# Group norm of layer 1 put ahead of the block turns on VectorE, its 1/std applied by ScalarE

## The chip, the cores and the metric

The kernel runs on one core of a Trainium2 chip. A core has five engines that each work through a queue of their own in order: TensorE (PE, matrix products; PEld is its weight load, which overlaps), VectorE (DVE), ScalarE (ACT), GpSimd (POOL) and SyncE (SP, which issues most transfers here). [...] The metric is the device time of one execution in microseconds; the median of 3 runs of the kernel before is 3231.37 us (3231.11 to 3235.41).

## What is computed

Two attention layers over an image x of 128 rows, 256 columns and 256 channels (with a batch of one). Each layer adds to x an attention over the columns of each row, computed from a group norm of x. Cut to what matters here:

```
def _gn(v, G=32, eps=1e-5):            # statistics over rows, columns and the 8 channels of a group
    g = v.reshape(B_, H_, W_, G, C_ // G)
    m = jnp.mean(g, axis=(1, 2, 4), keepdims=True)
    s = jnp.var(g, axis=(1, 2, 4), keepdims=True)
    return ((g - m) / jnp.sqrt(s + eps)).reshape(v.shape)

x = x + _L0_conv_ref(_gn(x), ...)      # 8 heads, layer norm, pair bias from z, gate
x = x + _L1_conv_ref(_gn(x), ...)      # 4 heads, scores only where |i - j| <= 16

def _L1_conv_ref(x, w_in, b_in, w_out, b_out, band):
    qkv = x2 @ w_in.T + b_in
    q, k, v = jnp.split(qkv, 3, axis=-1)
    ...                                # scores, softmax inside the band, times v
    return (out @ w_out.T + b_out).reshape(B, T, F, C)
```

The group norm of layer 1 needs mean and variance over the whole output of layer 0. So layer 1 can't begin its products before the last row of layer 0 is done: that point is the seam.

## The kernel before

Both layers go over the 128 rows in 64 pairs. Layer 0 stores its result in 16 blocks of 8 rows (`x1[j]`, stored from the tile `xo`, L1456, 2 MB each) and gathers the moments of each block on VectorE (L1471 to L1484) into `st1`, which holds mean and summed squares by partition and group.

Layer 1 works on one pair at a time, transposed, with channels on the partitions. For each pair four transfers on SP's queue bring `xs` (L1771) in such an order that a single VectorE transpose of 32x32 blocks turns it into `xT` (method `turn`, L1781); a fifth brings the rows as they are (`xt`, L1776) for the residual. `centre(k)` (L1786, on ScalarE, one for each half `k` of the channels) subtracts the mean and writes `xgT`, on which PE's products work; with the second half POOL adds the output bias to `xt` (L1788). The transfers of a pair are issued where its object is made, not where its methods are called.

At the seam, `norm1` makes the constants of the norm: VectorE spreads the group's mean over its channels (L1723), PE averages over the partitions (L1724), VectorE forms the variance (L1725 to L1727), PE turns mean and variance into columns with channels on partitions (L1732), VectorE adds eps and negates the mean (`R1c` L1736, `nM1` L1738), POOL raises to the power -1/2 (L1737). VectorE then multiplies `R1c` into the input weights `w_in`, six instructions (L1742): 1/std is applied through the weights, the mean through the data.

`mix_weights` (L1749 to L1752, POOL) forms four sums of blocks of the q and k weights, `wst`. The pairs from the second on compute q and k with seven products of 128x128 blocks in place of eight; `wst` is for these products (`product`, L1824), together with four sums of data, `dT`, which `differences` (L1795 to L1798, POOL) makes from `xgT`. The first pair is projected in the plain way (`project`, L1845).

The seam is written out by hand, and each engine takes its instructions in this order: both pairs made (their transfers issued), `now.turn()`, `nxt.turn()`, `norm1()`, the two `now.centre(k)`, `mix_weights()`, then four projections, two rows of values, `nxt.centre(k)` and `nxt.differences()`. After it comes the loop over the pairs; its first pass begins with `nn.turn()` for the third pair, and each pass ends with `n3.turn()`, the turn for two passes ahead. The tiles `wst`, `xs`, `xT`, `xgT` and `gn_each` lie in memory that layer 0 has used; `w_in`, `nM1` and `st1` are constants that stay in place.

Of the kernel before, what the change touches and what calls it, by code (L numbers as in the profile page):

```python
# [9 lines left out]
F32 = mybir.dt.float32  # L10
AF = mybir.ActivationFunctionType
ALU = mybir.AluOpType
# [4 lines left out]
P = 128  # L17
# [4 lines left out]
def bcast(ap, axis, n):  # L22

    ap = ap.unsqueeze(axis)
    shape = list(ap.shape)
    shape[axis] = n
    return ap.broadcast_to(shape)
# [746 lines left out]
def fast_kernel(  # L774
# [25 lines left out]
    nc = tc.nc  # L800
    S, I, C = x.shape
# [7 lines left out]
    KC = C // P  # L809
# [6 lines left out]
    const = ctx.enter_context(tc.tile_pool(name="const", bufs=1))  # L816
# [17 lines left out]
    def load_chunks(src, n, name):  # L834
        t = const.tile([P, src.shape[0] // P, n], F32, name=name)
        queued.append((t, src.rearrange("(k p) n -> p k n", p=P)))
        return t
# [90 lines left out]
    w_in = load_chunks(w_inT, 3 * C, "w_in")  # L928

    w_out = const.tile([P, KC, C], F32, name="w_out")  # L930
    for a in range(KC):
        for h in range(H1):
            n = P // H1
# [5 lines left out]
    for h in range(H1):  # L939
        n = P // H1  # L940
# [279 lines left out]
    class Pair:  # L1220
# [36 lines left out]
        def centre(self):  # L1257
            self.xg = la.tile([P, NT, C], F32, name="xg", tag="xg", bufs=1)
            nc.gpsimd.tensor_tensor(self.xg, self.xt, bcast(M0, 1, NT), ALU.subtract)
# [303 lines left out]
    behind, nx, n = None, 0, 0  # L1563
# [41 lines left out]
    with tc.manual_schedule():  # L1605
# [3 lines left out]
        for p in range(NP):  # L1609
# [52 lines left out]
            old, was, now, nxt, nn = was, now, nxt, nn, nn3  # L1662
# [41 lines left out]
    with tc.tile_pool(name="l1", bufs=2) as sb, tc.tile_pool(  # L1704
        name="l1s", bufs=4
    ) as sm, tc.tile_pool(name="ps1_s", bufs=4, space=PSUM) as ps_s, tc.tile_pool(
        name="ps1_o", bufs=1, space=PSUM
    ) as ps_o:

        def mm1(name):  # L1710
            return ps_s.tile([P, 512], F32, name=name, tag="s")

        nM1 = const.tile([P, KC], F32, name="nM1")
        wst = sb.tile([P, 4, 2, P], F32, name="wst", bufs=1)

        def norm1():

            each = sm.tile([P, 2, C], F32, name="gn_each", bufs=1)
            dev = sm.tile([P, C], F32, name="gn_dev", bufs=1)
            R1c = sm.tile([P, KC], F32, name="gn_R", bufs=1)  # L1720
            ps = [mm1("ps_gn") for _ in range(2)]
            by_group = lambda a: a.rearrange("p (g e) -> p g e", e=GE)
            nc.vector.tensor_copy(by_group(each[:, 0, :]), bcast(st1[:, :, 1], 2, GE))  # L1723
            nc.tensor.matmul(ps[0][:, :C], avg, each[:, 0, :], start=True, stop=True)  # L1724
            nc.vector.tensor_tensor(dev, each[:, 0, :], ps[0][:, :C], ALU.subtract)  # L1725
            nc.vector.tensor_mul(dev, dev, dev)
            nc.vector.scalar_tensor_tensor(  # L1727
                by_group(each[:, 1, :]), bcast(st1[:, :, 2], 2, GE), 1.0 / (S * NB * GE), by_group(dev), ALU.mult, ALU.add
            )
            for n in range(2):  # L1730
                for k in range(KC):
                    nc.tensor.matmul(  # L1732
                        ps[1][:, 2 * n + k : 2 * n + k + 1], each[:, n, k * P : (k + 1) * P], avg[:, 0:1],
                        start=True, stop=True,
                    )
            nc.vector.tensor_scalar_add(R1c, ps[1][:, 2:4], 1e-5)  # L1736
            nc.gpsimd.tensor_tensor(R1c, R1c, mhalf[:, :KC], ALU.pow)  # L1737
            nc.vector.tensor_scalar_mul(nM1, ps[1][:, 0:2], -1.0)  # L1738
            for n in range(3):
                for k in range(KC):  # L1740
                    at = slice(n * C, (n + 1) * C)
                    nc.vector.tensor_scalar_mul(w_in[:, k, at], w_in[:, k, at], R1c[:, k : k + 1])  # L1742

        def mix_weights():

            a = [[w_in[:, k, 0 : 2 * C].rearrange("p (n m c) -> p m n c", n=2, m=KC)[:, m] for k in range(KC)]
                 for m in range(KC)]
            s1, s2, s3, s4 = (wst[:, n] for n in range(4))
            nc.gpsimd.tensor_tensor(s1, a[1][0], a[1][1], ALU.add)  # L1749
            nc.gpsimd.tensor_tensor(s2, s1, a[0][0], ALU.subtract)  # L1750
            nc.gpsimd.tensor_tensor(s3, a[0][0], a[1][0], ALU.subtract)
            nc.gpsimd.tensor_tensor(s4, a[0][1], s2, ALU.subtract)  # L1752
# [9 lines left out]
        class Pair1:  # L1762
# [20 lines left out]
            def centre(self, k):  # L1783
                if k == 0:
                    self.xgT = sb.tile([P, KC, N2], F32, name="xgT1", tag="xgT")
                nc.scalar.activation(self.xgT[:, k, :], self.xT[:, k, :], AF.Identity, bias=nM1[:, k : k + 1])  # L1786
                if k == KC - 1:
                    nc.gpsimd.tensor_tensor(self.xt, self.xt, bcast(bout_r, 1, 2 * NB), ALU.add)  # L1788

# [167 lines left out]
        def pair1(p):  # L1957
            return Pair1(p) if p < NP else Nobody()
# [14 lines left out]

        with tc.manual_schedule():
            now, nxt = pair1(0), pair1(1)
            now.turn()
            nxt.turn()
            norm1()
            for k in range(KC):
                now.centre(k)  # L1980
            mix_weights()
            for m in range(KC):
                now.project("qT", m)
                now.project("kT", m)
            for r in range(2):
                now.values(r)
            for k in range(KC):
                nxt.centre(k)
            nxt.differences()
# [6 lines left out]
        with tc.manual_schedule():  # L1996
            was = Nobody()
            for p in range(NP - 1):
# [42 lines left out]
                was, now, nxt = now, nxt, nn  # L2041
# [19 lines left out]
        ps = mm1("ok_ps")  # L2061
# [4 lines left out]
@with_exitstack  # L2066
def mixer_kernel(ctx, tc, *args):

    nc = tc.nc
    keep = ctx.enter_context(tc.tile_pool(name="verdict", bufs=1))  # L2070
    verdict = keep.tile([1, 1], mybir.dt.int32, name="verdict")
    fast_kernel(tc, *args, verdict)
    again = nc.values_load(verdict[0:1, 0:1], min_val=0, max_val=1)
    with tc.If(again > 0):
        general_kernel(tc, *args)
# [53 lines left out]
```

## Time and profile before

| | before |
|---|---|
| median of 3 runs | 3231.37 us (3231.11 to 3235.41) |
| profiled execution, its own time | 3251.55 us |
| its span, first to last instruction | 3249.8 us |
| busy in the span | PE 95%, DVE 72%, POOL 66%, ACT 47% |
| mean granted PE clock | 0.982 |
| last block of layer 0 stored (x<-xo issued, landed) | 2051.12, 2058.18 us |
| first projection of layer 1 on PE | 2078.93 us |
| first scores of layer 1 on PE | 2090.88 us |

Times of single instructions count from the start of the span. A line of the profile names the engine, the line of the kernel, the operation and the tiles (written `out<-in`, with buffer numbers and trailing digits left out: `nM` is `nM1`, `xs<-x` is a load from `x1`); `xN` counts instructions that stand merged. In brackets stands how long the engine was idle before, and who released it. The profiled execution took 20.2 us more than the runs' median, so differences are formed within the profile and carried over to the median.

### The profile page before, as it was taken

To read this page: it belongs to the slowest core of one execution; us is meant where nothing else is said; L and a number is where in the kernel's file an instruction comes from. 1 tells how busy PE (TensorE), PEld (TensorE's weight loads), DVE (VectorE), ACT (ScalarE), POOL (GpSimd) and SP (SyncE) were. 2 spreads that over 40 slices of the span, in tenths; PEclk is the share of its full clock that TensorE was granted. 3 is DMA by queue.
4 is the path that set the end of the run, shared out by engine and by line. 5 is a ranking of instruction groups with operands and counts; after the bars stand their busy time and mean duration, and the time that the engine had idled before them with its cause. 6 is when DMAs were issued, how large, how long until landed. Compare 5 with 4: busy or idle time off the path is not lost.

```text
span 3249.8 us, 82756 instructions
## 1 busy us (share of the span) xinstructions
PE 3073.5 (95%) x34916; PEld 2066.9 (64%) x34916; DVE 2339.4 (72%) x3684; ACT 1537.5 (47%) x2501; POOL 2157.6 (66%) x1631
## 2 busy tenths in 40 slices
PE   5379999999999999999999999699999999999998
PEld 3245555555555555555555555488888888888886
DVE  7966676777777777777777777577766666666676
ACT  2255444444444444444444444255555555555553
POOL 3368888888888887888788886355454555545453
PEclk9799999999999999999999999899999999999999
DMA  9953333434433442344343332533334334343431
GB/s 349 391 150 63 65 88 86 95 70 96 95 95 70 95 91 64 87 92 95 70 95 96 67 88 70 106 80 89 92 88 92 91 90 95 85 100 86 94 93 47
DMA packets 726973, 329.10 MB, mean 101 GB/s; under 512 B 574560, under 2 KB 675808, under 8 KB 725440
## 3 DMA queue, kind: packets, MB, share of 16 engines
q1 hardware_dynamic: 721520, 320.81, 40.3%
q8 instruction: 277, 4.54, 0.7%
q10 hardware_dynamic: 5072, 2.90, 0.3%
q14 instruction: 104, 0.85, 0.1%
HBM read 254.88 MB, written 68.75 MB: 100 GB/s over the span
## 4 chain that ended last, share of the span: by engine, by line
PE 71%; DMA 12%; DVE 8%; POOL 4%; issue 2%; ACT 1%; SPq 1%; ACTq 0%; DVEq 0%; POOLq 0%
PE ps_p L1322 13%; PE ps_qk L1824 11%; PE ps_v L1860 7%; PE ps_su_y L1943 7%; PE ps_sc L1356 6%; PE ps_y L1443 5%; PE ps_ov L1388 5%; PE ps_v L1337 5%; PE ps_o L1903 3%; DMA rvb<-rsum 3%; PE ps_sc L1874 3%; DMA rs_d<-lrs 3%; DMA rsum<-rv 3%; PE ps_su L1396 2%; POOL eboth L1377 2%
## 5 line engine op out<-in xcount | busy, mean ns | idle before, releaser
L1377 POOL TENSOR_TENSOR eboth<-e 128x512 f32<-128x512 f32 x512 | 639.4, 1272 | 214.8 <-DVE e L1372 214.7
L1363 ACT ACTIVATE ps_sc<-ps_sc 128x1024 f32<-128x1024 f32 x512 | 492.8, 1006 | 575.9 <-PE ps_sc L1356 575.9
L1372 DVE TENSOR_TENSOR e<-ps_sc,eb 128x1024 f32<-128x1024 f32 x512 | 602.9, 1219 | 221.8 <-ACT ps_sc L1363 219.2
L1885 POOL TENSOR_TENSOR e<-e,bw 128x384 f32<-128x384 f32 x256 | 252.7, 1008 | 520.3 <-ACT e L1883 520.3
L1356 PE MATMUL ps_sc<-qT,kT 32*128 32x256 f32 x4096 | 293.3, 400 | 2.0 <-ACT kT L1326 2.0
L1443 PEld LDWEIGHTS ps_y<-wo,oT 128*128 128x128 f32 x1024 | 190.8, 190 | 106.6 <-POOL oT L1433 51.1
L1443 PE MATMUL ps_y<-wo,oT 128*128 128x256 f32 x1024 | 246.2, 383 | 12.8 <-POOL oT L1433 11.5
L1322 PE MATMUL ps_p<-xnT,wq 128*128 128x512 f32 x512 | 254.8, 619 | 2.6 <-POOL xnT L1309 2.3
L1309 POOL TENSOR_TENSOR xnT<-xgT,rs_r 128x512 f32<-128x512 f32 x128 | 160.1, 1273 | 135.4 <-DMA rs_r<-rs_d 133.2
L1943 PE MATMUL ps_su_y<-w_out,oT 128*128 128x256 f32 x1024 | 245.9, 384 | 3.8 <-DVE odd L1921 2.8
L1337 PE MATMUL ps_v<-wv,xnT 128*128 128x256 f32 x1024 | 248.6, 386 | 0.0
L1388 PE MATMUL ps_ov<-e,v 128*32 128x256 f32 x4096 | 247.7, 382 | 0.0
L1356 PEld LDWEIGHTS ps_sc<-qT,kT 32*128 32x128 f32 x4096 | 184.9, 184 | 94.4 <-issue 82.6
L1829 ACT ACTIVATE u<-ps_qk,bin_c 128x256 f32<-128x256 f32 x378 | 177.7, 478 | 141.2 <-PE ps_qk L1824 133.2
L1322 PE MATMUL ps_p<-xnT,wk 128*128 128x512 f32 x512 | 240.6, 592 | 0.0
L1860 PE MATMUL ps_v<-w_in,xgT 128*128 128x256 f32 x1024 | 238.3, 386 | 0.0
L1337 PEld LDWEIGHTS ps_v<-wv,xnT 128*128 128x128 f32 x1024 | 189.3, 190 | 76.8 <-issue 56.9
L1322 PE MATMUL ps_p<-xgT,wg 128*128 128x512 f32 x512 | 236.8, 605 | 0.0
L1922 DVE RECIPROCAL rv<-odd 128x256 f32<-128x256 f32 x128 | 224.4, 1753 | 4.4
L1943 PEld LDWEIGHTS ps_su_y<-w_out,oT 128*128 128x128 f32 x1024 | 196.4, 192 | 32.3 <-DVE odd L1921 3.6
L1860 PEld LDWEIGHTS ps_v<-w_in,xgT 128*128 128x128 f32 x1024 | 189.3, 190 | 32.8 <-issue 0.5
L1824 PE MATMUL ps_qk<-dT,wst 128*128 128x256 f32 x756 | 191.4, 389 | 5.2 <-DVE qT L1835 5.1
(198 smaller groups left out, 5694.3 us busy)
## 6 DMA issues: line engine op xcount, KB each, us to landing
xa<-in_x_dram SPq DMA_DIRECT2D x8, 4096.0 KB
xt<-in_x_dram SPq DMA_DIRECT2D x64, 512.0 KB
x<-xo SPq DMA_DIRECT2D x16, 2048.0 KB
xs<-x SPq DMA_DIRECT2D x256, 128.0 KB
xt<-x SPq DMA_DIRECT2D x64, 512.0 KB
xs<-in_x_dram SPq DMA_DIRECT2D x252, 128.0 KB
rvb<-rsum SPq DMA_DIRECT2D x252, 128.0 KB
out_dram<-yo SPq DMA_DIRECT2D x63, 512.0 KB
```

What stands on the lines that cost most here:

```text
L1322: nc.tensor.matmul(ps, w[:, k, m * P : (m + 1) * P], getattr(self, src)[:, k, :], start=(k == 0), stop=(k == KC - 1),)
L1337: nc.tensor.matmul(self.ps_v[:, b * C : (b + 1) * C], self.xnT[:, k, t * P : (t + 1) * P], wv[:, k, :], start=(k == 0), stop=(k == KC - 1),)
L1356: nc.tensor.matmul(self.pss[q // 2][:, q % 2, b, :], self.kT[rs, c, r * I + b * P : r * I + (b + 1) * P], self.qT[rs, c, r * I : (r + 1) * I],
L1363: nc.scalar.activation(self.pss[a], self.pss[a], AF.Exp)
L1372: nc.vector.tensor_tensor(e, pss[a], eb[:, h : h + 2], ALU.mult)
L1377: nc.gpsimd.tensor_tensor(t, es[a][:, :, 0, :], es[a][:, :, 1, :], ALU.add)
L1388: nc.tensor.matmul(ov[q * D0 : (q + 1) * D0, c, :], self.v[:, r, b, h * D0 : (h + 1) * D0], es[q // 2][:, q % 2, b, :], start=(b == 0), st ...
L1443: nc.tensor.matmul(self.ps_y[:, b * C : (b + 1) * C], self.oT[r][:, k, b * P : (b + 1) * P], wo[:, k, :], start=(k == 0), stop=(k == KC - 1),)
L1824: nc.tensor.matmul(to, lhs, rhs, start=start, stop=True, skip_group_check=True)
L1860: nc.tensor.matmul(ps[:, b * C : (b + 1) * C], self.xgT[:, k, t * P : (t + 1) * P], w_in[:, k, 2 * C : 3 * C], start=(k == 0), stop=(k == ...
L1885: nc.gpsimd.tensor_tensor(e[:, q], e[:, q], bcast(bw.rearrange("p b w -> p (b w)"), 1, KC), ALU.mult)
L1943: nc.tensor.matmul(ps[:, b], self.oT[r][:, k, b * P : (b + 1) * P], w_out[:, k, :], start=(k == 0), stop=(k == KC - 1),)
```

## The change

`R1c` becomes a constant tile. `norm1` no longer scales `w_in`; instead `nM1` becomes minus the mean times 1/std, in one instruction which reads `R1c` after POOL's power. `centre` gives ScalarE the scale `R1c` beside the bias `nM1`, so 1/std is applied to the data. `mix_weights` and `norm1` go ahead of both turns, and the second pair's turn goes behind the first pair's two centres.

```
         nM1 = const.tile([P, KC], F32, name="nM1")
+        R1c = const.tile([P, KC], F32, name="R1c")
...
-            R1c = sm.tile([P, KC], F32, name="gn_R", bufs=1)
...
             nc.vector.tensor_scalar_add(R1c, ps[1][:, 2:4], 1e-5)
             nc.gpsimd.tensor_tensor(R1c, R1c, mhalf[:, :KC], ALU.pow)
-            nc.vector.tensor_scalar_mul(nM1, ps[1][:, 0:2], -1.0)
-            for n in range(3):
-                for k in range(KC):
-                    at = slice(n * C, (n + 1) * C)
-                    nc.vector.tensor_scalar_mul(w_in[:, k, at], w_in[:, k, at], R1c[:, k : k + 1])
+            nc.vector.scalar_tensor_tensor(nM1, ps[1][:, 0:2], -1.0, R1c, ALU.mult, ALU.mult)
...
-                nc.scalar.activation(self.xgT[:, k, :], self.xT[:, k, :], AF.Identity, bias=nM1[:, k : k + 1])
+                nc.scalar.activation(
+                    self.xgT[:, k, :], self.xT[:, k, :], AF.Identity,
+                    bias=nM1[:, k : k + 1], scale=R1c[:, k : k + 1],
+                )
...
             now, nxt = pair1(0), pair1(1)
+            mix_weights()
+            norm1()
             now.turn()
-            nxt.turn()
-            norm1()
             for k in range(KC):
                 now.centre(k)
-            mix_weights()
+            nxt.turn()
             for m in range(KC):
```

## The prediction

> **What bounds the kernel now.** I read the page first (slices, then the chain of waits), then busy time by stretches, then the instructions around the seam in order of time. On the page, PE is full in both layers. Layer 0 ends and layer 1 begins in slice 26 of 40 (2031 to 2112 us), where PE falls to 6 tenths.
>
> ```profile
> span 3249.8 us, 82756 instructions
> PE   5379999999999999999999999699999999999998
> ```
>
> By stretches (columns: length; busy us of PE, PEld, DVE, ACT and POOL, each with its count; granted PE clock; DMA share; GB/s):
>
> ```profile
> 2050.00:2079.00 29.00, 3.29 (x13) 2.63 (x11) 12.01 (x34) 1.33 (x2) 3.02 (x2) 0.58 0.98 223
> 2112.00:2400.00 288.00, 283.30 (x5036) 232.64 (x5036) 223.62 (x307) 147.30 (x313) 151.89 (x143) 1.00 0.37 86
> 2400.00:2800.00 400.00, 400.00 (x7008) 333.59 (x7010) 269.57 (x385) 211.59 (x451) 208.80 (x200) 1.00 0.41 93
> ```
>
> From 2112 on PE is busy 98 to 100%, so what starts the loop earlier ends the kernel earlier by as much, unless something else then binds. Between 2050 and 2079 PE does almost nothing. What it waits for is in the order of time there (start, length, engine, line; in brackets the idle time before it and its releaser):
>
> ```profile
> 2051.12 0.38 SPq L1456 DMA_DIRECT2D x<-xo  x1
> 2055.18 0.19 DVE L1484 SCALAR_TENSOR_TENSOR st<-gd,st 128x32 f32<-128x32 f32 x1
> 2058.45 2.75 SPq L1771 DMA_DIRECT2D xs<-x  x4
> 2064.48 1.25 DVE L1781 STREAM_TRANSPOSE xT<-xs 128x1024 f32<-128x1024 f32 x1 [9.10 <-DMA xs<-x]
> 2069.93 1.25 DVE L1781 STREAM_TRANSPOSE xT<-xs 128x1024 f32<-128x1024 f32 x1 [4.21 <-DMA xs<-x]
> 2071.10 0.25 DVE L1723 COPY gn_each<-st 128x256 f32<-128x256 f32 x1
> 2072.79 0.42 DVE L1725 TENSOR_TENSOR gn_dev<-gn_each,ps_gn 128x256 f32<-128x256 f32 x1 [1.44 <-PE ps_gn L1724]
> 2073.24 0.42 DVE L1726 TENSOR_TENSOR gn_dev<-gn_dev 128x256 f32<-128x256 f32 x1
> 2075.61 0.71 POOL L1737 TENSOR_TENSOR gn_R<-gn_R,mhalf 128x2 f32<-128x2 f32 x1 [35.51 <-DVE nM L1738]
> 2076.29 2.34 POOL L1788 TENSOR_TENSOR xt<-xt,bout_r 128x1024 f32<-128x1024 f32 x1
> 2076.36 4.21 DVE L1742 TENSOR_SCALAR w_in<-w_in,gn_R 128x256 f32<-128x256 f32 x6 [0.90 <-POOL gn_R L1737]
> 2078.93 8.57 PE L1845 MATMUL ps_p<-xgT,w_in 128*128 128x512 f32 x16 [3.73 <-DVE w_in L1742]
> 2079.65 0.77 POOL L1749 TENSOR_TENSOR wst<-w_in 128x256 f32<-128x256 f32 x1 [1.02 <-DVE w_in L1742]
> 2080.48 1.23 DVE L1781 STREAM_TRANSPOSE xT<-xs 128x1024 f32<-128x1024 f32 x1
> ```
>
> The reader is to see a serial chain on DVE in front of PE: first pair's data, turn(0), a 4.21 us wait for the second pair's data, turn(1), only then the group norm, then the weights' scaling. The statistics st were complete at 2055.4. DVE idles 9.10 us before turn(0), longer than the whole norm.
>
> [...] (1) [...] six scalings of w_in took 340 ns each but for the first, 2425 ns (the tile's longest); it began 0.07 us after POOL's xt addition and let PE go 0.2 us after that ended. (2) [...] with bias alone (L1786) 718 ns, with scale and bias (L1252, same shape) 802 ns, so 84 ns is used:
>
> ```profile
> L1252 ACT ACTIVATE xgT<-xgT,col 128x512 f32<-128x512 f32 x126 | 95.0, 802 | 0.0
> L1786 ACT ACTIVATE xgT<-xT,nM 128x512 f32<-128x512 f32 x128 | 91.7, 718 | 39.9 <-DVE nM L1738 39.9
> ```
>
> (3) [...] ps_p matmuls start 0.86 us apart for four, then 0.43.
>
> **The change part by part.** PE's first projection stood at 2078.93. I rebuild when it starts.
>
> *norm1 moved ahead of both turns.* It issues on DVE, PE and POOL, no DMA; SP's queue keeps its order. Its tile gn_each lies in layer 1's memory, as does xs; xs reads rows stored long before, yet SP held it until x<-xo landed at 2058.18. So I take norm1 to be held to 2058.2 too (lower bound 2055.4, statistics done; no gain from that, since turn(0) waits for its data to 2064.48 anyway). COPY would start at 2058.5; from COPY to the first reader of the pow it took 2071.10 to 2076.36 = 5.26, so 2063.75.
>
> *nM1 now waits for the pow* (scalar_tensor_tensor in place of tensor_scalar, about 0.19 by L1484): done 2063.95. Queued behind it on DVE are turn(0) and turn(1); ACT and PE wait for those. Slack to 2064.48: 0.5.
>
> *mix_weights moved ahead of the pow on POOL*: four instructions, 0.77+3x0.73 = 2.95, into layer-1 memory (wst), so they too start at 2058.4, and are done at 2061.35 if nothing blocks. On POOL they pass only the pow and the two xt additions; the pow is wanted at 2063. [...] POOL first: COPY waits for the first (+0.7), then runs 2059.2; gn_dev 2060.9; its square[...] wants 2061.35 and gets in at 2061.7 when the last ends. From square to reader of the pow 2073.24 to 2076.36 = 3.12, so 2064.8, nM1 done 2065.0. Bounds: no blocking 2063.95 (turn(0) unmoved); COPY behind all four, 2061.35+5.26+0.19 = 2066.8 (turn(0) 2.3 late). I take 2065.0, 0.5 late, by the order above.
>
> *Six w_in scalings removed*: PE waited for two of them; the other four had cover. The 2.44 us that they put on the path are gone. wst comes from unscaled weights, the same algebra.
>
> *centre with a scale pointer*: turn(0) 2065.0 to 2066.25; ACT some 0.15 later (0.24 from nM to the first centre before, where ACT still had a layer's first waits to clear); k=0 takes 0.80: 2067.2; PE 0.1 later (0.06 from centre to ps_qk at 2092.2): 2067.3. Gain 2078.93-2067.3 = 11.6. The same sum by what leaves the path between turn(0)'s end, 2065.73, and 2078.93: 5.45 of wait and turn for the second pair, 5.2 of norm, 2.6 of scaling with its hand-over to PE, together 13.2; what comes in is 0.5 of lateness, 0.15, 0.80 and 0.1, together 1.55. The second pair's two centres add 2x0.084 = 0.17 on the path ACT, dT, PE in the loop's first pass. The other 124 lie beside PE: exp after centre(0) waits 0.2 for PE, after centre(1) 1.4, both over 0.084; the sum if that cover were gone is 124x0.084 = 10.4.
>
> *nxt.turn moved after centre*: one DVE instruction, still limited by data (2069.93 to 2071.2); its reader nxt.centre runs after the value copies, near 2080. Hidden by 8 us.
>
> *R1c moved to the constants*: no instruction.
>
> *Clock*: at other starts from idle the half-clock transposes lasted some 3.6 to 4.4 us (3.4 here); 0.4 longer at half rate is 0.2 lost. [...]
>
> Sum: 11.6-0.17-0.2 = 11.3 us. Profiled: span 3249.8 to 3238.5, execution 3251.55 to 3240.2. The runs' median is 20.2 below the profiled execution and I subtract the same there: 3231.37-11.3 = 3220.1.
>
> What is late next: pair 2's turn was at 2080.48 just behind the scalings, so its data was there by then; the joins that it would hold are wanted near 2082.5, with the turn done at 2081.7. Pair 3's xs was issued to 2079.98; the second pair's xs landed 3.7 after its last issue, so 2084 is an estimate; its turn (2105.33 before) is wanted near 2094.
>
> **Rivals.**
> A (0.73): as worked out, 3220.1; from no blocking and an equal clock (-12.0) to 1 us worse.
> B (0.17): [...] COPY behind all four, 1.8 beyond my sum, and a longer cold clock, 0.5: -9.0, 3222.4. For: the 2425 ns. [...]
> C (0.05): hidden anyway: the loop starts earlier but pairs 2 and 3 come no sooner (the DMA share is 0.98 until 2079, so no transfer can come much earlier than it did). If turn(pair 3) stays at 2105.33 all 11.3 is lost: 3231.4. Against: the slacks above.
> D (0.02): the scale pointer lies on the path in each pair, -11.3+10.4: 3230.5. Against: ACT's waits for PE.
> E (0.03), slower: R1c takes room among the constants, so the tiles placed above them move by 32 bytes, xa among them, the 33.5 MB that the DMA-bound start loads; at 413 GB/s (90 to 110 us) that is 81 us. If the new offset costs a quarter, +20.3-11.3: 3240.4; it decides from 14% on. For: DMA is full there. [...] That the change doesn't act is excluded: it reorders queues that obey it.
>
> **How the numbers follow.** 0.2% (6.5 us) is about what a measurement of this kernel can tell from no change. Faster A+B = 0.90; same C+D = 0.07; slower 0.03. Range: A and B with the run's scatter, 3217.5 (-12.0 and 1.9 of scatter, from 4.3 over the three runs) to 3224.5[...].
>
> **What would show it.** norm1's COPY right after x<-xo lands; POOL's wst beside it; nM1's end against xs landing at 2064.4 (B if it is above 2066); turn(0) directly before centre; centre at 0.80; PE's ps_p at about 2067; the same 18.5 us per pair after. A stall of DVE for xs in the first two passes means C; exp waiting for centre means D; a longer stretch up to 200 us means E. PE's ps_p later than 2070 would make the forecast wrong.

## The result and the profile after

| | before | after |
|---|---|---|
| median, 6 runs each on one chip | 3231.53 us (3229.77 to 3237.17) | 3210.36 us (3209.41 to 3214.3) |
| ratio after to before, 95% interval | | 0.9932 (0.9922 to 0.9942) |
| profiled execution, span | 3251.55, 3249.8 us | 3210.37, 3208.6 us |
| from the last block's store (issue) to the first projection | 27.81 us | 15.75 us |
| a pass of layer 1's loop, with a range check of 512 columns | 18.46 us | 17.80 us |
| a pass without | 17.80 us | 17.80 us |

The kernel became 21.2 us faster (by the interval 18.7 to 25.2 us), where 11.3 had been forecast. The two spans differ by 41.2 us, 20 more than the runs do, and those 20 have nothing to do with the change: the last block of layer 0 was issued at 2051.12 us before and at 2031.64 us after, and layer 0's code is the same in both. A second profile of the changed kernel, on another chip (c1_after below), has it at 2052.97. So everything below is counted from that store.

On the page of the changed kernel the seam's slice (the 26th) has risen from 6 to 7:

```profile
span 3208.6 us, 82751 instructions
PE   5379999999999999999999999799999999999998
```

By stretches, each shifted by the 19.5 us that the store came earlier (the columns are those of the prediction):

```profile
2030.50:2059.50 29.00, 15.35 (x44) 9.25 (x42) 10.59 (x32) 4.85 (x7) 8.22 (x7) 0.71 0.95 222
2092.50:2380.50 288.00, 288.00 (x5187) 240.39 (x5176) 219.38 (x313) 154.89 (x325) 162.52 (x149) 1.00 0.41 92
```

The first line is the forecast gain: PE works 15.35 us of the seam's 29 and not 3.29. The second line was not forecast: in the loop's first 288 us PE is busy all the time, where it had 283.30, and does 151 matmuls more.

The seam in order of time:

```profile
2031.64 0.38 SPq L1456 DMA_DIRECT2D x<-xo  x1
2035.70 0.19 DVE L1484 SCALAR_TENSOR_TENSOR st<-gd,st 128x32 f32<-128x32 f32 x1
2038.94 0.72 POOL L1745 TENSOR_TENSOR wst<-w_in 128x256 f32<-128x256 f32 x1 [18.32 <-DMA x<-xo]
2039.17 0.64 DVE L1723 COPY gn_each<-st 128x256 f32<-128x256 f32 x1 [3.28 <-DMA x<-xo]
2041.10 0.72 POOL L1748 TENSOR_TENSOR wst<-w_in,wst 128x256 f32<-128x256 f32 x1
2041.70 0.42 DVE L1726 TENSOR_TENSOR gn_dev<-gn_dev 128x256 f32<-128x256 f32 x1
2043.93 0.71 POOL L1737 TENSOR_TENSOR R1c<-R1c,mhalf 128x2 f32<-128x2 f32 x1 [2.11 <-DVE R1c L1736]
2044.67 0.16 DVE L1738 SCALAR_TENSOR_TENSOR nM<-ps_gn,R1c 128x2 f32<-128x2 f32 x1 [0.82 <-POOL R1c L1737]
2045.04 1.25 DVE L1777 STREAM_TRANSPOSE xT<-xs 128x1024 f32<-128x1024 f32 x1 [0.21 <-DMA xs<-x]
2046.52 1.52 ACT L1782 ACTIVATE xgT<-xT,nM,R1c 128x512 f32<-128x512 f32 x2 [30.20 <-DMA xt<-x]
2047.39 8.96 PE L1844 MATMUL ps_p<-xgT,w_in 128*128 128x512 f32 x16 [3.74 <-ACT xgT L1782]
2050.60 1.25 DVE L1777 STREAM_TRANSPOSE xT<-xs 128x1024 f32<-128x1024 f32 x1 [4.31 <-DMA xs<-x]
2058.85 1.25 DVE L1777 STREAM_TRANSPOSE xT<-xs 128x1024 f32<-128x1024 f32 x1 [7.00 <-DMA xs<-x]
```

The reader is to see that norm1's COPY and POOL's wst both wait for x<-xo to land, as forecast; that COPY is stretched from 0.25 to 0.64 us beside POOL; and that nM1 is done at 2044.83, so the first turn still waits 0.21 us for its data and starts 13.40 us after the store (13.36 before). The second pair's wait of 4.31 us stands beside PE's projections. The third pair's wait of 7.00 us is the sign that I had named for case C, but it stood in time that DVE had free: the turn was done at 2060.10, and DVE's next instruction, a join, waited for PE:

```profile
2063.08 0.42 DVE L1834 TENSOR_TENSOR qT<-ps_qk,u 128x256 f32<-128x256 f32 x1 [2.99 <-PE ps_qk L1823]
```

Where the 21.7 us between the two profiles' stores and ends come from, each item read off as the difference of two starts:

| stretch | before | after | gain |
|---|---|---|---|
| store to first projection | 27.81 | 15.75 | 12.06 |
| to first scores | 11.95 | 12.35 | -0.40 |
| to the first out_dram store (first two passes) | 32.59 | 33.21 | -0.62 |
| to the issue of the last pair's first out_dram store | 1115.21 | 1106.52 | 8.69 |
| to the end | 11.12 | 9.13 | 1.99 |

The last item is nearly all PE's clock: the eight products of the very last row took 3.78 us at a granted clock of 0.50 before and 1.99 us at 1.00 after. It isn't shown to be the change's, since c1_after, the same kernel in another profile, took 3.78 us as before, and 10.97 for the item (the first line is after's, the second c1_after's):

```profile
3199.50 1.99 PE L1942 MATMUL ps_su_y<-w_out,oT 128*128 128x256 f32 x8 [1.18 <-DVE yo L1946]
3222.67 3.78 PE L1942 MATMUL ps_su_y<-w_out,oT 128*128 128x256 f32 x8 [0.99 <-DVE yo L1946]
```

The 8.69 are 12 passes of 0.66 (7.9) and 0.8 more, 0.5 of it in the last passes. These 0.8 aren't shown to be the change's either: c1_after took 1107.23 us for this stretch, 0.7 more than after.

All 12 are passes with a range check of 512 columns. A range check is three DVE instructions (L958 to L960) that test a tile that is in memory already, such as `eb`, against two bounds; its result is needed at the very end only. The loop runs one at the end of a pass, as long as there are any. Beside it POOL multiplies the exponentials `e` by the band mask `bw`, and behind it on DVE's queue stands the join `qT`, which adds up partial products for PE. The thirteenth check in the loop, of the mask's 256 columns, costs nothing either way (17.80 in both); two more run in the last passes. One of the 12 before the change:

```profile
2142.21 0.74 POOL L1798 TENSOR_TENSOR dT<-xgT,dT 128x256 f32<-128x256 f32 x1
2142.90 2.14 POOL L1885 TENSOR_TENSOR e<-e,bw 128x384 f32<-128x384 f32 x2
2142.98 1.20 DVE L958 TENSOR_SCALAR chk<-eb 128x512 f32<-128x512 f32 x1
2145.63 0.69 DVE L960 TENSOR_REDUCE ok<-chk 128x1 f32<-128x512 f32 x1
2146.23 0.42 DVE L1835 TENSOR_TENSOR qT<-ps_qk,u 128x256 f32<-128x256 f32 x1
2146.70 1.99 PE L1824 MATMUL ps_qk<-dT,wst 128*128 128x256 f32 x8 [0.39 <-DVE qT L1835]
```

and the like pass after it:

```profile
2109.75 0.73 POOL L1795 TENSOR_TENSOR dT<-xgT,dT 128x256 f32<-128x256 f32 x1 [0.32 <-ACT xgT L1782]
2111.80 0.39 DVE L958 TENSOR_SCALAR chk<-eb 128x512 f32<-128x512 f32 x1
2111.82 2.63 POOL L1884 TENSOR_TENSOR e<-e,bw 128x384 f32<-128x384 f32 x2
2113.87 2.98 PE L1823 MATMUL ps_qk<-dT,wst 128*128 128x256 f32 x12
2114.23 0.42 DVE L1834 TENSOR_TENSOR qT<-ps_qk,u 128x256 f32<-128x256 f32 x1
```

Before, POOL's band mask began 0.08 us ahead of DVE's check, and the check's first instruction took 1.20 us. After, the check begins 0.02 us ahead of the mask and takes 0.39 us; now POOL's two mask instructions are the longer ones (2.63 in place of 2.14). The join qT comes 2.43 us after the check's start and not 3.25, and PE, which waited for it before, doesn't wait.

The single instructions show that the later of the two stands still. Before, POOL's first mask instruction ended at 2143.90 and the check's first instruction at 2144.19. In all 13 checks of 512 columns of `eb` and `sums` in before, in e1 and in e3 that instruction ended 0.28 or 0.29 us after POOL's, and it takes 0.38 us when it comes first.

POOL's lateness comes from ScalarE: centre with a scale pointer takes 91 ns more (809 in place of 718), POOL's dT waits for centre (POOL's idle time ahead of dT, ended by xgT, is 0.32 us here and 0.24 in the like pass before), and the mask stands behind dT on POOL's queue.

```profile
L1782 ACT ACTIVATE xgT<-xT,nM,R1c 128x512 f32<-128x512 f32 x128 | 103.3, 809 | 30.2 <-DMA xt<-x 30.2
```

### The profile page after: what moved, and what is told of

Read it like the earlier page. It is cut to its first block, busy times and chain, and to the rows that moved or that the text cites. A ratio compares the mean times of both kernels' runs of the same rounds, so it can differ in the third digit from the quotient of the medians.

```text
span 3208.6 us, 82751 instructions
## 1 busy us (share of the span) xinstructions
PE 3058.2 (95%) x34916; PEld 2069.3 (64%) x34916; DVE 2310.3 (72%) x3678; ACT 1548.8 (48%) x2501; POOL 2165.7 (67%) x1631
## 4 chain that ended last, share of the span: by engine, by line
PE 90%; DVE 4%; DMA 4%; ACT 1%; issue 0%; POOL 0%; SPq 0%; ACTq 0%; DVEq 0%; POOLq 0%
PE ps_p L1322 21%; PE ps_qk L1823 13%; PE ps_sc L1356 8%; PE ps_v L1859 7%; PE ps_ov L1388 7%; PE ps_v L1337 7%; PE ps_su_y L1942 7%; PE ps_y L1443 7%; PE ps_o L1902 4%; PE ps_sc L1873 3%; PE ps_su L1396 3%; PE ps_su_y L1902 2%; DVE st L1178 1%; DVE zst L1103 1%; DMA zt<-in_z_dram 1%; DMA bv_c<-in_b_in_dram 1%
## 5 line engine op out<-in xcount | busy, mean ns | idle before, releaser
L1884 POOL TENSOR_TENSOR e<-e,bw 128x384 f32<-128x384 f32 x256 | 259.7, 1035 | 498.8 <-ACT e L1882 498.8
L1309 POOL TENSOR_TENSOR xnT<-xgT,rs_r 128x512 f32<-128x512 f32 x128 | 160.6, 1276 | 72.7 <-DMA rs_r<-rs_d 65.7
L1343 DVE TENSOR_TENSOR v<-ps_v,vb_r 128x512 f32<-128x512 f32 x128 | 88.3, 690 | 149.5 <-PE ps_v L1337 149.4
```

The source lines that it names most:

```text
L1884: nc.gpsimd.tensor_tensor(e[:, q], e[:, q], bcast(bw.rearrange("p b w -> p (b w)"), 1, KC), ALU.mult)
```

## The experiments

Theory L: of DVE's check and POOL's mask the one that comes second stands still (the check's first instruction takes 1.20 us in place of 0.39), 91 ns on ScalarE turn their order, and this gives the loop's gain, 7.9 of its 8.7 us; the seam gives the rest. Rivals: T, passes get shorter because the loop starts earlier against its transfers; M, because memory moved by 32 bytes; A, because a longer ACT instruction helps in itself. The times of e1 to e5 and of the later runs stand on chips where the kernel before took 3251.5 to 3254.8 us; each is compared with it by the ratio.

**The scale pointer taken off the kernel after, and put on the kernel before.** e1:

```
                     self.xgT[:, k, :], self.xT[:, k, :], AF.Identity,
-                    bias=nM1[:, k : k + 1], scale=R1c[:, k : k + 1],
+                    bias=nM1[:, k : k + 1],
```

> The kernel after with ScalarE's scale pointer taken off again: centre subtracts only, and the factor 1/std is left out of layer 1's input. Theory L[...]: the 84 ns that the pointer adds to each centre put POOL's band mask behind DVE's range check[...], and without them each of the 13 passes with a check is 18.46 us long again and not 17.80; the seam keeps its gain. 3210.4 + 8.7 - 0.3 = 3218.8 us, passes with a check 18.46. Rival T (the loop's passes are shorter because it begins earlier against its transfers) and rival M (because memory moved by 32 bytes): the passes stay at 17.80, 3210 us.

Measured: ratio to before 0.9963 (0.9949 to 0.9977), some 12 us below it and so 9 to 10 short of the kernel after; 15.57 us from store to first projection; 12 passes of 18.45 us are back (the 13 expected counted the mask's check, which costs nothing). The check's first instruction takes 1.20 us again, started 0.08 us behind the mask:

```profile
2128.68 2.13 POOL L1884 TENSOR_TENSOR e<-e,bw 128x384 f32<-128x384 f32 x2
2128.76 1.20 DVE L958 TENSOR_SCALAR chk<-eb 128x512 f32<-128x512 f32 x1
```

e2:

```
                     self.xgT[:, k, :], self.xT[:, k, :], AF.Identity,
-                    bias=nM1[:, k : k + 1],
+                    bias=nM1[:, k : k + 1], scale=ones[:, 0:1],
```

> The kernel before, whose seam is left as it is, with a scale pointer to a column of ones on every centre: 84 ns more on ScalarE, the same result. Theory L: passes with a check fall from 18.46 to 17.80 us, 3231.5 - 8.7 + 0.2 = 3223.0 us. Rivals T and M: no pass gets shorter, 3231.7 us.

Measured: 0.9972 (0.9961 to 0.9984), by the ratio 9.1 us below before (6.4 by the medians; in its profile the seam took 1.4 us longer); no pass over 17.81 in the checks' stretch; the check 0.38 us. With the old seam, the old start of the loop and the old memory layout the passes are short, and with the new ones but no pointer they are long. So neither the loop's start (T) nor the memory layout (M) makes them short.

**POOL later, ScalarE untouched.** e3 and e5 put memsets ahead of the mask:

```
                     nc.scalar.activation(ev[:, q], ps[q][:, : KC * NK // 2 * W], AF.Exp)
+                if r == 0:
+                    for _ in range(3):        # e3: one, without the loop
+                        nc.gpsimd.memset(mhalf[:, 63:64], -0.5)
```

> The kernel before with one tiny POOL instruction (a memset of one column) ahead of the band mask of each first row: POOL's mask comes later with nothing changed on ScalarE. Theory L: if the memset takes 0.1 us or more, [...] passes with a check 17.80 us, about 3223 us. Rivals T and M, and also the rival that a longer ACT instruction itself helps PE: 3231.5 us.

Measured: 0.9996 (0.9988 to 1.0005), no gain, as both rivals had it. By theory L the dose was too small: the memset of 0.09 us moved the mask by only 0.05 us (why not by more, the profile doesn't show), and POOL was still ahead, by 0.03 us:

```profile
2142.13 0.09 POOL L1885 MEMSET mhalf<- 128x1 f32 x1
2142.19 2.13 POOL L1887 TENSOR_TENSOR e<-e,bw 128x384 f32<-128x384 f32 x2
2142.22 1.25 DVE L958 TENSOR_SCALAR chk<-eb 128x512 f32<-128x512 f32 x1
```

e5 takes three memsets for a larger dose:

> The kernel before with three tiny POOL memsets in place of the one of e3, ahead of the band mask of each first row. One put the mask 0.04 us later, which was not enough: POOL was still 0.03 us ahead of the check. Three put it some 0.15 us later. Theory L: now the check comes first, its first instruction takes 0.39 us and not 1.2, passes with a check 17.80 us, 8.5 us below the kernel before. Rival A (it is the longer ACT instruction that helps, not POOL's lateness): passes with a check 18.5, the time of the kernel before.

Measured: 0.9972 (0.9962 to 0.9982), passes 17.80:

```profile
2142.85 0.68 POOL L1886 MEMSET mhalf<- 128x1 f32 x3
2142.95 0.38 DVE L958 TENSOR_SCALAR chk<-eb 128x512 f32<-128x512 f32 x1
2143.37 0.69 DVE L959 SCALAR_TENSOR_TENSOR chk<-eb,chk 128x512 f32<-128x512 f32 x1
2143.49 2.39 POOL L1888 TENSOR_TENSOR e<-e,bw 128x384 f32<-128x384 f32 x2
```

Work added to POOL makes the kernel 9 us faster, with no ACT instruction changed, so A falls too.

**DVE later in the kernel after.** e4:

```
                 if checks and p > 0:
+                    nc.vector.memset(ok[:, 31:32], 1.0)
                     checks.pop(0)()
```

> The kernel after with one tiny DVE instruction (a memset of one column) ahead of each check: the check comes later by about 0.06 to 0.2 us, while POOL's mask stays. Theory L: [...] the check's first instruction takes 1.2 us in place of 0.39, and passes with a check are 18.46 us or a little more, 3210.4 + 8.7 = 3219 us. Rivals T and M: 3210.5 us, since 0.1 us more on DVE is nothing.

Measured: 0.9965 (0.9953 to 0.9977), passes with a check of `eb` 18.55 us. 0.06 us of memset cost 0.75 us in each of them:

```profile
2128.47 1.29 DVE L958 TENSOR_SCALAR chk<-eb 128x512 f32<-128x512 f32 x1
2128.49 2.13 POOL L1884 TENSOR_TENSOR e<-e,bw 128x384 f32<-128x384 f32 x2
2128.50 0.06 DVE L2039 MEMSET ok<- 128x1 f32 x1
```

The records' starts alone don't name the winner here (the check's record starts before that of the memset ahead of it); the 1.29 us do, which again end 0.28 us after POOL's first mask instruction. In two of the four checks of `sums` in e4 DVE still came first: their first instruction took 0.42 us, and their passes 17.80.

**The seam taken apart.** e6 puts now.turn() ahead of norm1() again, e7 both turns:

```
             mix_weights()
+            now.turn()
+            nxt.turn()                # e7 only; in e6 it stays behind centre
             norm1()
-            now.turn()
             for k in range(KC):
                 now.centre(k)
-            nxt.turn()                # e7 only
```

> The kernel after with the first pair's turn ahead of norm1 on DVE again (the second pair's turn and mix_weights stay as they are). Theory of the seam, as predicted: the norm no longer fits into the wait for the first pair's data, so from the issue of the last block's store to PE's first projection it takes 15.75 + 5.4 = 21.2 us; 5.4 us above the kernel after, 15.8 below the kernel before. Rival X (PE's start is set by the transfers and the second turn alone): 15.75 and no difference to the kernel after.

> The kernel after with both turns ahead of norm1 on DVE, so of the seam only the scalings of w_in stay removed. Theory of the seam: 15.75 + 10.8 = 26.5 us from the store to the first projection; 10.8 above the kernel after, 10.4 below the kernel before, of which 8.7 are the loop's. Rival X: 15.75 + 5.4 for the wait for the second pair's data alone, 5.4 us above the kernel after.

Measured: 20.56 us from store to projection in e6 (15.75 after), 26.54 in e7; ratios 0.9948 (0.9935 to 0.9962) and 0.9968 (0.9956 to 0.9981). So of the seam's 12.06 us, 4.8 are the norm inside the first wait (5.4 had been expected), 6.0 the second pair's wait and turn out of the path, and the last 1.3 the scalings of w_in less the pointer's and hand-over costs. Rival X, that the transfers and the second turn alone set PE's start, falls.

**Further on: the wait for the store.** What holds the seam now is memory: layer 1's tiles wait for all that layer 0 held. In the kernel after the statistics are done 4.25 us after the last block's store is issued, and norm1's COPY starts at 7.53, released by the store's landing. c1_after is the kernel after on the chip of e8 and e10.

> The kernel after as it is, so that the next two are compared with it on the same chip: 21 us below the kernel before (ratio 0.9932), 15.75 us from the issue of the last block's store to the first projection.

Measured: 3232.74 us, 0.9934 (0.9922 to 0.9947), 15.70 us from store to projection.

```
-    with tc.tile_pool(name="l1", bufs=2) as sb, tc.tile_pool(
-        name="l1s", bufs=4
+    with tc.tile_pool(name="l1", bufs=2, reuse_waits="tile") as sb, tc.tile_pool(
+        name="l1s", bufs=4, reuse_waits="tile"
...
-        def norm1():
+        def norm1(meanwhile):
...
             nc.tensor.matmul(ps[0][:, :C], avg, each[:, 0, :], start=True, stop=True)
+            meanwhile()
...
-            norm1()
-            now.turn()
+            norm1(now.turn)
```

> The kernel after with layer 1's two memory pools waiting tile by tile for the memory that they take over, not for everything that layer 0 held there, and the first pair's turn put into the norm, where DVE waits for PE. If the wait for the last block's store is what holds the seam now, norm1 starts when the statistics are done (4.1 us after the store's issue, not 7.5) and the first projection comes some 3 us earlier, 12.5 in place of 15.75: 3 us below the kernel after. Rival: the first pair's transfers stand behind the store on SP's queue and share the DMA engines with its 2 MB, so they land no earlier and nothing is gained.

Measured: projection at 17.34 and not 12.5; 0.9953 (0.9939 to 0.9966), no gain over the kernel after. The norm's COPY did start 4.3 us after the store and not 7.5. But the rival was nearly right: the transfers, issued from 0.4 us after the store on, were there 11.7 us after it, 1.7 sooner than in the kernel after and not 3. The turn inside the norm made it worse, since the norm's next step stands behind the turn on DVE's queue and waited with it for the data: PE's average for gn_dev was done at 2061.01, and gn_dev began at 2067.87, right behind the turn:

```profile
2055.04 0.38 SPq L1456 DMA_DIRECT2D x<-xo  x1
2055.47 7.48 SPq L1768 DMA_DIRECT2D xs<-x  x4
2066.70 1.25 DVE L1778 STREAM_TRANSPOSE xT<-xs 128x1024 f32<-128x1024 f32 x1 [7.03 <-DMA xs<-x]
```

e8 is e9 with the norm as in the kernel after (only the two pools' waits changed):

> As e9 (waits tile by tile), but with the first pair's turn behind the norm as in the kernel after, since in e9 the turn stood waiting for its data inside the norm and held it up. The data landed 11.7 us after the store's issue there, 1.7 earlier than in the kernel after: turn to 12.9, first projection at 14.0, 1.7 us below the kernel after. Rival (nothing gained, the store's 2 MB hold the transfers): 15.7.

Measured: projection at 13.78, as expected, but 0.9933 (0.9921 to 0.9945), which can't be told from c1_after, though the seam is 1.9 us shorter.

e10 is e9 with the last block's store on ScalarE's queue:

```
-                nc.sync.dma_start(
+                (nc.scalar if s == S - 1 else nc.sync).dma_start(
                     x1[j].rearrange("s (p b) c -> p s (b c)", b=NB), ...
```

> As e9 (waits tile by tile, the first pair's turn inside the norm), and the store of the last block issued from ScalarE's queue, where nothing stands at that time, so that SP can issue the first pair's transfers before it. If the transfers behind the store are what holds e9, the data are there before the statistics, the norm runs from 4.3 to 9.8 us after the store's issue with the turn inside its wait for PE, and the first projection stands at 10.9: 4.9 us below the kernel after, 26 below the kernel before. Rival (the memory of the first pair's tiles comes free no earlier, or the transfers are slow for another reason): 15 to 17 us and no gain over the kernel after.

Measured: projection at 10.54; 3228.95 us, 0.9924 (0.9912 to 0.9936), 3.8 us below c1_after by medians where 4.9 were expected, and the intervals overlap. Part was given back ahead of the store: mix_weights, no longer held, ran into layer 0's last merges and rows. e8 and e9 gave back too: from the start of the last but one merge (L1481) to the store's issue it took 10.9 us in c1_after, 14.7 in e8, 13.5 in e9 and 14.7 in e10. In e10, where the granted clock was 0.68 from 2043 to 2047:

```profile
2038.62 0.72 POOL L1746 TENSOR_TENSOR wst<-w_in 128x256 f32<-128x256 f32 x1
2038.74 0.65 DVE L1481 SCALAR_TENSOR_TENSOR gd<-gd 128x32 f32<-128x32 f32 x1
2046.74 5.95 PE L1443 MATMUL ps_y<-wo,oT 128*128 128x256 f32 x16 [0.78 <-DVE oT L1430]
```

e12 is e10 with mix_weights() behind norm1(now.turn):

> As e10, with mix_weights behind the norm on POOL. In e10 its four instructions, free of the wait for memory, ran into layer 0's last rows: DVE's merges with two SBUF inputs took 0.65 us in place of 0.2, rv came 0.8 us later, and PE fell to half clock for the last products (5.95 us in place of 3.72). Theory L: with them out of the way those stretches are back at 0.2 and 3.7 us, the first projection stays 10.5 us behind the store's issue, and the kernel is 2 to 3 us below e10, about 26 us below the kernel before (ratio 0.992 or less). Rival (the half clock in e10 was chance or came from the earlier transfers): no change to e10, ratio 0.9925.

Measured: 3227.57 us beside 3254.76 for the kernel before, 0.9907 (0.9894 to 0.9921), projection at 10.55:

```profile
2044.56 0.19 DVE L1481 SCALAR_TENSOR_TENSOR gd<-gd 128x32 f32<-128x32 f32 x1
2051.02 3.72 PE L1443 MATMUL ps_y<-wo,oT 128*128 128x256 f32 x16 [0.78 <-DVE oT L1430]
```

The merge is back at 0.19 and the rows at 3.72 us. From the merge to the store it takes 10.9 us again. This kernel is 27 us below the one before. Its interval lies below that of the kernel after (0.9922 to 0.9942, in c1_after 0.9922 to 0.9947) by a hair, but the two weren't run side by side, so that it beats the kernel after is likely and not shown. Against e10 the intervals overlap; what mix_weights gave back is shown by the lines and not by the times.

## Why the prediction was wrong

- *norm1 ahead of both turns, mix_weights beside it.* Right, and nearly in size: 11.6 forecast for the first projection, 12.06 measured. POOL came first, by 0.23 us, and COPY lost 0.4 us (0.64 in place of 0.25), as chosen; the second stop, of the square behind POOL's last sum, didn't show (0.42 us as before), so nM1 was done 13.2 us after the store and not 13.9, and the 0.5 us of lateness fell away: turn(0) stayed where it was, as in the bound without blocking (nM1 was 0.4 us later than that bound has it). One reading was short: the sixth scaling, too, took 808 ns and not 340, beside POOL's first sum. No sum of the forecast rests on it.
- *Scalings removed, nxt.turn moved, third pair's turn.* Right: e7 shows what is left when only the scalings go. The second and third pair's data came beside other work. Case C's sign showed, a DVE stall of 7.00 us for xs, but nothing waited behind it, so case C didn't happen; the sign was too loose.
- *Clock.* 0.2 us forecast, 0.4 measured up to the first scores, 1.0 in c1_after (12.95 us in place of 11.95). The projections began at a granted clock of 0.50, for 2.95 us before and for 3.70 us after, and went on at 1.00. The upper end of the forecast's range, 3224.5, also holds an estimate of mine for the clock that no run shows. The 2.0 us at the very end, where the last row ran at a granted clock of 1.00, are chance as far as is known: they are there in after and not in c1_after.
- *centre with a scale pointer.* This is the step that failed. It said: "The other 124 lie beside PE", because exp had 0.2 and 1.4 us of slack on ScalarE. That was true of ScalarE's own queue, and exp did stay hidden. It left out who else waits for centre: POOL's dT and, behind it on POOL's queue, the mask, which met DVE's check (0.08 us ahead of it before, 0.02 us behind it after). Its term was 0 in the forecast and +10.4 in case D; the run shows 7.9 us of gain in 12 passes, in a stretch that gained 8.7. With the 11.3 that is 19.2 to 20.0 of the 21.2 us measured. e1, e2, e4 and e5 show it from both sides. That this came out as a gain is luck: nothing in the change aims at the order of mask and check, and 0.06 us of memset on DVE takes it away again (e4).
- *What bounds the kernel.* I read "98 to 100%" off the stretches and took the loop for full. The stretch of 283.30 in 288 us held the loop's gain, and asking what its 4.7 idle us were (0.39 us for each of the 12 checks) would have led to qT behind the check. Only a part of the 7.9 us shows as idle time. I had read at the seam what it costs DVE to start just behind POOL (2425 ns in place of 340 for a scaling of w_in), and didn't look for such a meeting in the loop.

The third row of the split, 0.6 us lost in the first two passes, I can place only in part: 0.18 in the second pair's two centres, as forecast (0.17; e2, the kernel before with a pointer alone, loses the same 0.18 there), and 0.29 in an idle gap of PE for which the profile shows no releaser (0.86 in c1_after).

## What to carry to other kernels

In this kernel DVE's check and POOL's mask started within a tenth of a microsecond of each other, and an edit that moved either by as little was priced by who came first (0.66 to 0.75 us a pass), not by its own length. Look for such pairs of starts before calling an added instruction free. Follow a lengthened instruction to every engine that waits for it, and to what stands behind that on the queue. And a stretch that is 98% busy is not a full one: ask for the 2%, when they repeat in a dozen passes.

## What the runs showed of the hardware

- Adding 0.06 us to DVE cost 0.75 us per pass with a check (e4), and adding three POOL memsets, 0.68 us together, won 0.66 us per such pass (e5).
- Of the check and the mask, the one that came second stood still until the other's instruction was done, and then took nearly its usual time. POOL's two mask instructions took 2.63 us behind the check (after) and 2.14 ahead of it (before). The check's first instruction ended 0.28 or 0.29 us after POOL's (0.38 alone), its second, L959, 0.55 us after POOL's (0.69 alone). The second took 1.37 us before and after alike, since a mask instruction stood ahead of it in both, and 0.69 in e5, where it began 0.12 us ahead of the mask. A merge of layer 0 (L1481) took 0.65 us beside POOL's wst in e10, and 0.19 in e12, where wst came later.
- A short overlap didn't show: the norm's square (L1726) took 0.42 us, as before, though it began 0.12 us before POOL's last sum ended. By the numbers just given the first 0.10 to 0.14 us of a DVE instruction (0.38 less 0.28, 0.69 less 0.55) pass before it has to stand still; this is an estimate.
- The first sixteen projections took 8.6 to 9.9 us over the fourteen profiles, without order by kernel. Their first 2.95 us in before and 3.70 us in after ran at a granted clock of 0.50, the rest at 1.00.
- Layer 0 with the same code took 20 us more or less from one profile to another, as the kernel before took 3231.5 us on the first chip and 3251.5 to 3254.8 on those of the experiments. The cause stays open; what differs is a wait for a transfer: POOL's wait for rs_r was 65.7 us in all in the faster profile, 133.2 and 135.5 us in the slower ones of before and c1_after.
